# Column sums of the second attention layer as two float32r products in another PSUM bank, the next batch's half-size sums issued apart, and the first batch's copies all on ScalarE

## The chip, the cores and the metric

The kernel runs on one NeuronCore of a Trainium2 chip. The metric is the device time of one execution in microseconds (us), given as the median of several runs. Engines are named as the profile names them: PE is TensorE (PEld its weight loads), DVE is VectorE, ACT is ScalarE, POOL is GpSimd, and SP is the engine whose queue issues most DMAs.

## The reference, cut to what matters

The input x is (8, 32, 32, 512) in float32: 8 batches of N = 1024 tokens with C = 512 channels. Two layers follow one another, each with a residual and a GroupNorm of 32 groups ahead of it.

```python
# layer 0: 16 heads of 32
qkv = (_gn(x) @ w_qkv)                       # q, k, v: 512 columns each
attn = softmax((q * 32**-0.5) @ k.T)         # per head, 1024 x 1024
x = x + (attn @ v) @ w_proj + b_proj
# layer 1: 4 heads of 128, with relative position logits
q, k, v = _gn(x) @ Wq / sqrt(128), _gn(x) @ Wk, _gn(x) @ Wv
scores = q @ k.T + relative_logits(q, pos_emb_w, pos_emb_h)
x = x + (softmax(scores) @ v) @ Wo
```

All of it is in float32. A softmax needs, for each query, the sum of the exponentials over 1024 keys; these sums are what the first part of the change is about.

## The kernel before

Activations lie transposed, channels on the partitions (`x0T`, `x1T`, four chunks of 128 channels). The 512x512 weight products are done in a Winograd form of seven products in place of eight: `forms` (L324) makes four half-size sums of the activation (`f_...`, each a DVE operation over 128x1024 elements, L332 to L335), `Matrix.add_up` (L146) makes the matching sums of the weights (`prep_...`), and `seven` runs the products, always cut into quarters of 32 columns (L312, so 16 issues make one product of 512).

Two batches are in flight. In loop b `side_by_side` (L862) steps through the first layer's attention of batch b (`attention_0`: scores L532, exponential L540 on ACT, accumulation L551, sums of exponentials L562 on DVE) and, by a running cost, hands out pieces of the other work between its steps: the output product of batch b-1's first layer, of batch b-2's second, the projections of batch b-1's second layer, its attention, and the projections of batch b+1. The second layer's attention has cost 0, so that it runs in one piece inside one step of the first layer's attention. Only in the last loop, b = 7, where no batch comes after, are the first 32 of its 64 steps for batch 6 spread among first-layer steps; and in the round after it batch 7's second layer runs with nothing beside it. The loading and normalising of batch b+1 (`load`) is woven into the second layer's attention: from its fourth step on, a piece at every sixth (L970). Its last piece is `forms`.

`attention_1` (L637) goes through 64 steps a batch: 4 heads h, 2 halves c of the queries, 8 blocks j of 128 keys. A step puts the scores into a bank (`ps`: L647 in full precision, L648, the position part, in float32r), takes the exponential on ACT (L650), multiplies it by v into the accumulator (L659), and adds it to the running sum `es` on DVE (L668, L670). The products of a step and the accumulation of the step before alternate. After eight steps ACT copies the accumulator to `q` (L673), and `finish` makes the sums over the partitions, by one full-precision product of an all-ones matrix and `es` (L679), into one of the three banks that the scores and the accumulator also use. `normalise` copies it (L495, ACT), takes reciprocals by way of two transposes (L497 to L513, DVE), and multiplies (L517, POOL). A batch has eight such finishes: seven are issued within the next group's first step, the last at once.

[...] four hold the first layer's scores (tag `ps`), one its accumulator (`acc`), three are those of `bank`. The framework's list scheduler orders each engine's instructions from the program order and its estimates; `tc.issue_after` and `tc.keep_in_program_order` bind it where they stand.

The first batch is loaded apart (`load_first`, L719): rows come by DMA, PE transposes them, ACT and DVE copy the two halves of the tokens (h = 0, 1) into four chunks, DVE takes statistics of each chunk (L248, L249), `put_away` (L217) sends each chunk to DRAM for the residual, and `group_norm` takes the averages (L260 to L285 on DVE, the root L289 on POOL) and normalises in place (L292). `fetch` (L135) brings a 512x512 weight matrix for `add_up`; both it and the copies to DRAM are on SP's queue.

Of the kernel before, what the change touches and what calls it, by code (L numbers as in the profile page):

```python
# [9 lines left out]
F32 = mybir.dt.float32  # L10
F32R = mybir.dt.float32r
# [6 lines left out]
P = 128  # L18
# [9 lines left out]
def quick_path(  # L28
# [23 lines left out]
    nc = tc.nc  # L52
# [28 lines left out]
    def bank(name, shape=None):  # L81
        return psum.tile(shape or [P, NB], F32, tag="bank", name=name, bufs=3)
# [1 line left out]

    ident = consts.tile([P, P], F32, tag="ident", name="ident")
    make_identity(nc, ident)
    ones = consts.tile([P, P], F32, tag="ones", name="ones")
    nc.gpsimd.memset(ones, 1.0)
    bproj_sb = consts.tile([P, CC], F32, tag="bproj_sb", name="bproj_sb")
    with nc.allow_non_contiguous_dma(reason="512 values, once"):  # L90
        nc.gpsimd.dma_start(bproj_sb, b_proj.rearrange("(cc p) -> p cc", p=P))
# [212 lines left out]
    in_place = [False]  # L304

    half_done = [None]

    def by_columns(out, weights, moving, start, stop, open_sum=False):

# [11 lines left out]
                tc.keep_in_program_order(ins)  # L321
        in_place[0] = False

    def forms(x, name):  # L324


        a11, a12 = x[:, :HC, :NB], x[:, HC:, :NB]
        a21, a22 = x[:, :HC, NB:], x[:, HC:, NB:]
        s1, s2, s4 = [
            mem.tile([P, HC, NB], F32, tag=f"form{i}", name=f"f{i}_{name}", bufs=1) for i in (1, 2, 4)  # L330
        ]
        nc.vector.tensor_add(s1, a21, a22)  # L332
        nc.vector.tensor_sub(s2, s1, a11)  # L333
        nc.vector.tensor_sub(a21, a11, a21)
        nc.vector.tensor_sub(s4, a12, s2)  # L335
        return [a11, a12, s4, a22, s1, s2, a21]

    def snapshot(tag, name):
        return mem.tile([P, NB], F32, tag=tag, name=name, bufs=3 if tag == "e1" else 2)
# [294 lines left out]
                if i % 2:  # L634
                    yield 0

    def attention_1(q, k, v, posT, b):  # L637

        steps = [(h, c, j) for h in range(H1) for c in range(NH) for j in range(NT)]
        state = {}  # L640

        def front(h, c, j):
            name = f"1_{b}_{h}_{c}_{j}"
            ps = bank(f"ps_{name}")
            keys = slice(j * P, (j + 1) * P)
            queries = slice(c * NB, (c + 1) * NB)
            nc.tensor.matmul(ps, k[h][:, keys], q[:, h, queries], start=True, stop=False)  # L647
            nc.tensor.matmul(ps, sel_flat[:, keys], posT[:, h, queries], start=False, stop=True)  # L648
            e = mem.tile([P, NB], F32, tag="e1", name=f"e_{name}", bufs=3)
            nc.scalar.activation(e, ps, AF.Exp, scale=1.0 / math.sqrt(D1))  # L650
            return e

        def back(h, c, j, e):
            name = f"1_{b}_{h}_{c}_{j}"
            if j == 0:
                state["acc"] = bank(f"acc_{name}")
                state["first"] = e
            acc = state["acc"]
            nc.tensor.matmul(  # L659
                acc,  # L660
                v[:, j, h * D1 : (h + 1) * D1],
                e,
                start=(j == 0),
                stop=(j == NT - 1),
            )
            if j == 1:
                state["esum"] = mem.tile([P, NB], F32, tag="es1", name=f"es_{name}", bufs=2)
                nc.vector.tensor_add(state["esum"], state["first"], e)  # L668
            elif j > 1:
                nc.vector.tensor_add(state["esum"], state["esum"], e)  # L670
            if j < NT - 1:
                return
            nc.scalar.copy(q[:, h, c * NB : (c + 1) * NB], acc)  # L673
            state["ended"] = (h, c, state["esum"])

        def finish(h, c, esum):
            name = f"1_{b}_{h}_{c}"
            su = bank(f"sums_{name}")
            nc.tensor.matmul(su, ones, esum, start=True, stop=True)  # L679
            normalise(q[:, h, c * NB : (c + 1) * NB], su, name)  # L680

        pending = None
        for at in steps:
            e = front(*at)
            ended = state.pop("ended", None)
            if pending is not None:
                back(*pending)
            pending = (*at, e)
            if ended is not None:
                finish(*ended)  # L690
            yield 0
        back(*pending)
        yield 0
        finish(*state.pop("ended"))

    def load(b, st):

        x = xT = None
        parts = [(cc, h) for cc in range(CC) for h in range(NH)]
        ahead = [load_blocks(b, *parts[i]) for i in range(2)]  # L700
        for i, (cc, h) in enumerate(parts):
            xs = ahead.pop(0)
            if i + 2 < len(parts):
                ahead.append(load_blocks(b, *parts[i + 2]))
            if h == 0:
                yield 0
            if x is None:
                x = block(f"x0T_{b}")
                xT = chunks(x)
            nc.vector.transpose(xT[cc][:, h * NB : (h + 1) * NB], xs)  # L710
            if h == NH - 1:
                statistics(st, xT, cc, f"0_{b}")
        yield 0
        st["kept"] = put_away(xT, f"0_{b}")
        yield from group_norm(st, xT, f"0_{b}")
        st["xn"] = forms(x, f"xn0_{b}")
        yield 0

    def load_first(st):  # L719

        rows = block("x_rows", [P, NT, C])
        for t in range(NT):
            queue = nc.scalar if t % 2 else nc.sync
            queue.dma_start(rows[:, t, :], xf[0, t * P : (t + 1) * P, :])
        WV0.fetch(nc.sync)
        x = block("x0T_0")
        xT = chunks(x)
        for h in range(NH):
            if h == 0:
                whole = psum.tile([P, CC, NB], F32, tag="ps", name="turned_0", bufs=1)  # L730
                banks = [whole[:, cc, :] for cc in range(CC)]
            else:
                banks = [bank(f"turned_1_{cc}") for cc in range(CC - 1)]
                banks.append(psum.tile([P, NB], F32, tag="acc", name="turned_1", bufs=1))
            for t in range(NT // NH):
                for cc in range(CC):
                    nc.tensor.transpose(
                        banks[cc][:, t * P : (t + 1) * P],
                        rows[:, h * (NT // NH) + t, cc * P : (cc + 1) * P],
                        ident,  # L740
                    )
            for cc in range(CC):
                part = xT[cc][:, h * NB : (h + 1) * NB]
                if h == 0 or cc % 2:
                    nc.scalar.copy(part, banks[cc])
                else:
                    nc.vector.tensor_copy(part, banks[cc])

        idle = psum.tile([P, CC, NB], F32, tag="ps", name="idle", bufs=1)
        for t in range(6):  # L750
            nc.tensor.matmul(idle[:, t % CC, :], ident, rows[:, t, :], start=True, stop=True)
        for cc in (1, 0, 3, 2):
            statistics(st, xT, cc, "0_0")
        st["kept"] = put_away(xT, "0_0")
        run(group_norm(st, xT, "0_0"))
        st["xn"] = forms(x, "xn0_0")
# [101 lines left out]
    def run(part):  # L858
        for _ in part:
            pass  # L860
# [25 lines left out]
    def later(part, *args):  # L886

        yield from part(*args)
# [28 lines left out]
    WV0.add_up(nc.gpsimd, nc.gpsimd, keep=True)  # L917
    for m in (WQ0, WK0):
        m.fetch(nc.sync)
        m.add_up(nc.vector, nc.gpsimd, keep=True)  # L920
    fill_sel()
    stream = Stream(plan)

# [12 lines left out]
    for b in range(B + 1):  # L936
# [11 lines left out]
        if last is not None:  # L948
            norm = norm_1(b - 1, last, (lambda: half_done[0]) if past is not None else None)
            rest.append(after_0(b - 1, last, forms_past if past is not None else None))  # L950
            total += PRODUCT
            if past is not None:
                rest.append(woven(later(after_1, b - 2, past), norm, 3, 3))
                total += PRODUCT
            else:
                rest.append(chain([ALONE], (cost + ALONE for cost in norm), marked()))
                total += 4 * ALONE
            rest.append(later(second, b - 1, last))
            total += SECOND
            attention = later(lambda st: attention_1(*st.pop("at")), last)  # L960
            if here is not None and coming is None:

                attention = woven(
                    (int(at < H1 * NT) for at, _ in enumerate(attention)),
                    at_once(forms_0),
                    H1 * NT + NT,
                    H1 * NH * NT,
                )
                total += H1 * NT
            rest.append(woven(attention, incoming, 4, 6))  # L970
        else:
            rest.append(woven(rest_of_first(here), incoming, 0, 2))
            total += PRODUCT
# [502 lines left out]
```

## Time and profile before

| | |
|---|---|
| median of 9 runs | 3888.27 us (3885.27 to 3892.73) |
| the profiled execution | 3891.15 us, its span 3889.4 us |
| mean granted TensorE clock | 0.995 of full speed |
| PE busy | 3808.2 us, 98% of the span |
| DVE busy | 2514.8 us, 65% |
| ACT busy | 1724.4 us, 44% |
| POOL busy | 619.5 us, 16% |
| second-layer sums (L679) | 128 issues for 64 finishes |

The span is from the first to the last instruction of the profiled execution; the time holds what lies around it too. Busy shares are averages over stages with different limits. A group's line has the operation, its output and inputs with shapes, its count, the busy time and the mean of one in ns, and the idle time ahead of it with what ended it. A float32 product appears as two issues (x2) in the records. The records of PE overlap, since products are pipelined; the chain of waits cuts each piece where the next one starts.

### The profile page before, as it was taken

Reading aid. Unit: us, or ns where it says so; the run is one execution under the profiler, and the core shown is the slowest. Engines: PE = TensorE matmul, PEld = TensorE weight load, DVE = VectorE, ACT = ScalarE, POOL = GpSimd, SP = SyncE. Lnnn points to the kernel's source line nnn. Section 1 sums busy time; section 2 is a strip of 40 time slices with the busy share of each in tenths; the row PEclk is TensorE's granted clock in tenths of the full one; section 3 lists DMA queues with packets and bytes.
Section 4 is the critical chain, followed back from the end, with each engine's and each line's share of the span. In section 5 each row is a group of like instructions: output and inputs, shape, how many; then the busy total and the mean of one; then the engine's idle time right before and its main releaser. Section 6 shows DMA issues by size and latency. Waiting matters only on the chain. (4 is left out here: it accounts for less than half of the span.)

```text
span 3889.4 us, 79819 instructions
## 1 busy us (share of the span) xinstructions
PE 3808.2 (98%) x34478; PEld 1371.3 (35%) x34478; DVE 2514.8 (65%) x2905; ACT 1724.4 (44%) x1767; POOL 619.5 (16%) x400
## 2 busy tenths in 40 slices
PE   8999899999999999999999999999999999999998
PEld 3222244232442324432344323433234332334353
DVE  5767775577745867458674586646866568665544
ACT  2554553445434454344544445444453445553132
POOL 1341001121111210113110121111211112001101
PEclk9999999999999999999999999999999999999999
DMA  5231120133201422023220231202411033111401
GB/s 170 76 107 42 47 61 6 39 116 69 62 2 42 122 65 57 7 80 91 53 55 13 92 90 40 52 20 93 93 41 41 25 96 76 33 43 34 121 18 23
DMA packets 482984, 234.73 MB, mean 60 GB/s; under 512 B 269600, under 2 KB 461376, under 8 KB 481600
## 3 DMA queue, kind: packets, MB, share of 16 engines
q1 hardware_dynamic: 470992, 213.74, 20.4%
q0 software_dynamic: 2608, 13.70, 1.0%
q8 instruction: 274, 4.49, 0.5%
q10 hardware_dynamic: 9024, 2.10, 0.3%
q14 instruction: 86, 0.70, 0.1%
HBM read 170.72 MB, written 58.72 MB: 59 GB/s over the span
## 5 line engine op out<-in xcount | busy, mean ns | idle before, releaser
L540 ACT ACTIVATE e<-ps 128x2048 f32<-128x2048 f32 x512 | 961.6, 1878 | 838.2 <-PE ps L532 624.6
L562 DVE TENSOR_TENSOR es<-es,e 128x2048 f32<-128x2048 f32 x384 | 891.7, 2322 | 422.6 <-ACT e L540 419.9
L532 PE MATMUL ps<-q,k 32*64 32x512 f32 x8192 | 578.5, 617 | 27.1 <-ACT e L540 27.1
L650 ACT ACTIVATE e<-ps 128x512 f32<-128x512 f32 x512 | 305.7, 597 | 572.6 <-PE ps L648 539.2
L551 PE MATMUL acc<-e,v 128*32 128x512 f32 x4096 | 547.8, 606 | 0.0
L647 PE MATMUL ps<-q,k 128*128 128x512 f32 x1024 | 525.2, 594 | 0.3 <-DVE posT L633 0.3
L659 PE MATMUL acc<-e,v 128*128 128x512 f32 x1024 | 522.0, 593 | 0.0
L517 POOL TENSOR_TENSOR q<-q,su 128x512 f32<-128x512 f32 x128 | 213.4, 1668 | 1596.3 <-DVE su L513 1551.6
L670 DVE TENSOR_TENSOR es<-es,e 128x512 f32<-128x512 f32 x384 | 290.9, 758 | 250.9 <-ACT e L650 248.8
L648 PE MATMUL ps<-posT,sel 128*128 128x512 f32 x512 | 406.8, 795 | 0.0
L647 PEld LDWEIGHTS ps<-q,k 128*128 128x128 f32 x1024 | 192.9, 190 | 250.8 <-issue 244.5
L532 PEld LDWEIGHTS ps<-q,k 32*64 32x64 f32 x8192 | 120.5, 130 | 422.0 <-issue 220.4
L659 PEld LDWEIGHTS acc<-e,v 128*128 128x128 f32 x1024 | 193.5, 190 | 146.4 <-issue 105.1
L551 PEld LDWEIGHTS acc<-e,v 128*32 128x32 f32 x4096 | 81.8, 108 | 414.2 <-issue 368.2
L560 DVE TENSOR_TENSOR es<-e,e 128x2048 f32<-128x2048 f32 x64 | 173.9, 2717 | 38.0 <-ACT e L540 38.0
L497 DVE STREAM_TRANSPOSE tu<-su 128x512 f32<-128x512 f32 x128 | 90.6, 708 | 128.1 <-ACT su L495 128.0
L495 ACT COPY su<-sums 128x512 f32<-128x512 f32 x128 | 74.9, 585 | 150.4 <-PE sums L572 78.2
L648 PEld LDWEIGHTS ps<-posT,sel 128*128 128x128 f32 x512 | 97.5, 190 | 122.3 <-issue 122.3
L633 DVE TENSOR_TENSOR posT<-pp,posT 32x512 fp32r<-32x512 f32 x128 | 112.0, 875 | 32.0 <-ACT posT L628 30.7
L668 DVE TENSOR_TENSOR es<-e,e 128x512 f32<-128x512 f32 x64 | 44.2, 690 | 134.8 <-ACT e L650 134.8
L421 POOL TENSOR_TENSOR k<-b_k,p_k 128x512 f32<-128x512 f32 x32 | 51.2, 1600 | 482.0 <-ACT p_k L386 479.9
L628 ACT CAST posT<-pp 32x512 fp32r<-32x512 f32 x128 | 105.9, 827 | 45.9 <-PE pp L615 44.8
(195 smaller groups left out, 4454.2 us busy)
## 6 DMA issues: line engine op xcount, KB each, us to landing
w_qkv<-ws_qkv SPq DMA_DIRECT2D x168, 128.0 KB, 2.5
d<-x0T SPq DMA_DIRECT2D x32, 512.0 KB, 3.5
x1T<-d SPq DMA_DIRECT2D x32, 512.0 KB, 5.4
d<-x1T SPq DMA_DIRECT2D x32, 512.0 KB, 3.6
x2T<-d SPq DMA_DIRECT2D x32, 512.0 KB, 6.5
w_qkv<-in_L_conv_w_qkv SPq DMA_DIRECT2D x126, 128.0 KB, 2.2
out<-ot SPq DMA_DIRECT2D x240, 64.0 KB, 2.0
xs<-in_x SPq DMA_DIRECT2D x224, 64.0 KB, 2.5
```

The costliest lines, as they stand in the source:

```text
L517: nc.gpsimd.tensor_tensor(dst, dst, su, op=ALU.mult)
L532: nc.tensor.matmul(ps[some, r, :], k[m][rows, j * P + 64 * i : j * P + 64 * i + 64], q[m][rows, h * NB : (h + 1) * NB], start=True, stop=True,
L540: nc.scalar.activation(e, ps, AF.Exp, scale=D0 ** -0.5)
L551: nc.tensor.matmul(acc[r * D0 : (r + 1) * D0, :], v[:, j, c0 : c0 + D0], e[:, r, :], start=(j == 0), stop=(j == NT - 1),)
L560: nc.vector.tensor_add(state["esum"], state["first"], e)
L562: nc.vector.tensor_add(state["esum"], state["esum"], e)
L633: nc.vector.tensor_sub(rest, logits, greater)
L647: nc.tensor.matmul(ps, k[h][:, keys], q[:, h, queries], start=True, stop=False)
L648: nc.tensor.matmul(ps, sel_flat[:, keys], posT[:, h, queries], start=False, stop=True)
L650: nc.scalar.activation(e, ps, AF.Exp, scale=1.0 / math.sqrt(D1))
L659: nc.tensor.matmul(acc, v[:, j, h * D1 : (h + 1) * D1], e, start=(j == 0), stop=(j == NT - 1),)
L670: nc.vector.tensor_add(state["esum"], state["esum"], e)
```

## The change

Inside `attention_1` a finish becomes a generator. Its first part, issued right after the step in which the group's last addition stands, splits the running sum: ACT copies it rounded to float32r (`sg`), DVE subtracts that from it (`sr`). Three steps later two float32r products with the ones add `sg` and `sr` up, in the first of the four banks of the tag `ps`; `normalise` follows as before. At the end of a batch all parts run at once. Where the first layer's attention is stepped beside (the first 32 steps of batch 6), the first three finishes keep the old product and bank; they are now issued one place earlier, ahead of the next step's products.

`forms` is also to be had as a generator, `forming`. `load` uses it, each of the four sums a piece of its own, bound to be issued behind the newest addition to `es`; and since there are three more pieces, they are woven in at every fifth step for every sixth.

In `load_first` all copies go to ACT, in the order of chunks 0, 2, 1, 3, and the statistics follow that order. The weight sums of two matrices on DVE are bound behind the last of the first batch's half-size sums. In the built program this also moves a fetch of 1 MB (`prep_qkv`) ahead of the four copies to DRAM on SP's queue.

```diff
@@ -84,8 +84,9 @@
 
     ident = consts.tile([P, P], F32, tag="ident", name="ident")
     make_identity(nc, ident)
-    ones = consts.tile([P, P], F32, tag="ones", name="ones")
-    nc.gpsimd.memset(ones, 1.0)
+    ones_r = consts.tile([P, P], F32R, tag="ones", name="ones")
+    nc.gpsimd.memset(ones_r.bitcast(F32), 1.0)
+    ones = ones_r.bitcast(F32)
     bproj_sb = consts.tile([P, CC], F32, tag="bproj_sb", name="bproj_sb")
     with nc.allow_non_contiguous_dma(reason="512 values, once"):
         nc.gpsimd.dma_start(bproj_sb, b_proj.rearrange("(cc p) -> p cc", p=P))
@@ -304,6 +305,9 @@
     in_place = [False]
 
     half_done = [None]
+    last_form = [None]
+
+    added = [None]
 
     def by_columns(out, weights, moving, start, stop, open_sum=False):
 
@@ -321,7 +325,7 @@
                 tc.keep_in_program_order(ins)
         in_place[0] = False
 
-    def forms(x, name):
+    def forming(x, name, behind=None):
 
 
         a11, a12 = x[:, :HC, :NB], x[:, HC:, :NB]
@@ -329,11 +333,27 @@
         s1, s2, s4 = [
             mem.tile([P, HC, NB], F32, tag=f"form{i}", name=f"f{i}_{name}", bufs=1) for i in (1, 2, 4)
         ]
-        nc.vector.tensor_add(s1, a21, a22)
-        nc.vector.tensor_sub(s2, s1, a11)
-        nc.vector.tensor_sub(a21, a11, a21)
-        nc.vector.tensor_sub(s4, a12, s2)
+        for op, out, one, other in (
+            (nc.vector.tensor_add, s1, a21, a22),
+            (nc.vector.tensor_sub, s2, s1, a11),
+            (nc.vector.tensor_sub, a21, a11, a21),
+            (nc.vector.tensor_sub, s4, a12, s2),
+        ):
+
+            late = behind() if behind is not None else None
+            with tc.issue_after(late.ins) if late is not None else nullcontext():
+                last_form[0] = op(out, one, other)
+            yield 0
         return [a11, a12, s4, a22, s1, s2, a21]
+
+    def forms(x, name):
+        got = []
+
+        def whole():
+            got.append((yield from forming(x, name)))
+
+        run(whole())
+        return got[0]
 
     def snapshot(tag, name):
         return mem.tile([P, NB], F32, tag=tag, name=name, bufs=3 if tag == "e1" else 2)
@@ -634,7 +654,7 @@
                 if i % 2:
                     yield 0
 
-    def attention_1(q, k, v, posT, b):
+    def attention_1(q, k, v, posT, b, beside=0):
 
         steps = [(h, c, j) for h in range(H1) for c in range(NH) for j in range(NT)]
         state = {}
@@ -667,7 +687,7 @@
                 state["esum"] = mem.tile([P, NB], F32, tag="es1", name=f"es_{name}", bufs=2)
                 nc.vector.tensor_add(state["esum"], state["first"], e)
             elif j > 1:
-                nc.vector.tensor_add(state["esum"], state["esum"], e)
+                added[0] = nc.vector.tensor_add(state["esum"], state["esum"], e)
             if j < NT - 1:
                 return
             nc.scalar.copy(q[:, h, c * NB : (c + 1) * NB], acc)
@@ -675,23 +695,43 @@
 
         def finish(h, c, esum):
             name = f"1_{b}_{h}_{c}"
-            su = bank(f"sums_{name}")
-            nc.tensor.matmul(su, ones, esum, start=True, stop=True)
+            if (h * NH + c + 1) * NT < beside:
+                su = bank(f"sums_{name}")
+                nc.tensor.matmul(su, ones, esum, start=True, stop=True)
+                normalise(q[:, h, c * NB : (c + 1) * NB], su, name)
+                return
+
+            yield
+
+            greater = mem.tile([P, NB], F32R, tag="rec", name=f"sg_{name}", bufs=2)
+            nc.scalar.copy(greater, esum)
+            rest = mem.tile([P, NB], F32R, tag="rec", name=f"sr_{name}", bufs=2)
+            nc.vector.tensor_sub(rest, esum, greater.bitcast(F32))
+
+            yield
+            yield
+
+            su = psum.tile([P, HB, NB], F32, tag="ps", name=f"sums_{name}", bufs=1)[:, 0, :]
+            nc.tensor.matmul(su, ones_r, greater, start=True, stop=False)
+            nc.tensor.matmul(su, ones_r, rest, start=False, stop=True)
             normalise(q[:, h, c * NB : (c + 1) * NB], su, name)
 
         pending = None
+        ending = []
         for at in steps:
             e = front(*at)
-            ended = state.pop("ended", None)
             if pending is not None:
                 back(*pending)
             pending = (*at, e)
-            if ended is not None:
-                finish(*ended)
+            for part in ending:
+                next(part, None)
+            if "ended" in state:
+                ending = [finish(*state.pop("ended"))]
+                next(ending[0], None)
             yield 0
         back(*pending)
         yield 0
-        finish(*state.pop("ended"))
+        run(finish(*state.pop("ended")))
 
     def load(b, st):
 
@@ -713,8 +753,7 @@
         yield 0
         st["kept"] = put_away(xT, f"0_{b}")
         yield from group_norm(st, xT, f"0_{b}")
-        st["xn"] = forms(x, f"xn0_{b}")
-        yield 0
+        st["xn"] = yield from forming(x, f"xn0_{b}", lambda: added[0])
 
     def load_first(st):
 
@@ -739,17 +778,14 @@
                         rows[:, h * (NT // NH) + t, cc * P : (cc + 1) * P],
                         ident,
                     )
-            for cc in range(CC):
+            for cc in (0, 2, 1, 3):
                 part = xT[cc][:, h * NB : (h + 1) * NB]
-                if h == 0 or cc % 2:
-                    nc.scalar.copy(part, banks[cc])
-                else:
-                    nc.vector.tensor_copy(part, banks[cc])
+                nc.scalar.copy(part, banks[cc])
 
         idle = psum.tile([P, CC, NB], F32, tag="ps", name="idle", bufs=1)
         for t in range(6):
             nc.tensor.matmul(idle[:, t % CC, :], ident, rows[:, t, :], start=True, stop=True)
-        for cc in (1, 0, 3, 2):
+        for cc in (0, 2, 1, 3):
             statistics(st, xT, cc, "0_0")
         st["kept"] = put_away(xT, "0_0")
         run(group_norm(st, xT, "0_0"))
@@ -917,7 +953,9 @@
     WV0.add_up(nc.gpsimd, nc.gpsimd, keep=True)
     for m in (WQ0, WK0):
         m.fetch(nc.sync)
-        m.add_up(nc.vector, nc.gpsimd, keep=True)
+
+        with tc.issue_after(last_form[0].ins):
+            m.add_up(nc.vector, nc.gpsimd, keep=True)
     fill_sel()
     stream = Stream(plan)
 
@@ -957,8 +995,11 @@
                 total += 4 * ALONE
             rest.append(later(second, b - 1, last))
             total += SECOND
-            attention = later(lambda st: attention_1(*st.pop("at")), last)
-            if here is not None and coming is None:
+            shared = here is not None and coming is None
+            attention = later(
+                lambda st, steps: attention_1(*st.pop("at"), steps), last, H1 * NT if shared else 0
+            )
+            if shared:
 
                 attention = woven(
                     (int(at < H1 * NT) for at, _ in enumerate(attention)),
@@ -967,7 +1008,7 @@
                     H1 * NH * NT,
                 )
                 total += H1 * NT
-            rest.append(woven(attention, incoming, 4, 6))
+            rest.append(woven(attention, incoming, 4, 5))
         else:
             rest.append(woven(rest_of_first(here), incoming, 0, 2))
             total += PRODUCT
```

## Prediction

> **What bounds the kernel now.** I read the page's busy times first, then the windows inside the second layer's attention, the products by shape, the chain that ended last, and the timeline where one batch's attention ends. From the page:
>
> ```profile
> PE 3808.2 (98%) x34478; PEld 1371.3 (35%) x34478; DVE 2514.8 (65%) x2905; ACT 1724.4 (44%) x1767; POOL 619.5 (16%) x400
> ```
>
> TensorE is 98% of the span. Where the change acts it is everything (a window's TensorE busy us stand twice after its limits):
>
> ```profile
> 600.00:700.00 100.00, 100.00 (x351) 45.17 (x349) 47.06 (x76) 37.02 (x58) 9.07 (x6) 1.00 0.02 5
> ```
>
> The groups by shape show no idle ahead of any second-layer product worth naming (last number of the first three):
>
> ```profile
> L659 PE MATMUL acc<-e,v 128*128 128x512 f32 x1024 | 522.0, 593 | 0.0
> L648 PE MATMUL ps<-posT,sel 128*128 128x512 f32 x512 | 406.8, 795 | 0.0
> L679 PE MATMUL sums<-es,ones 128*128 128x512 f32 x128 | 65.4, 592 | 0.0
> ...
> L633 DVE TENSOR_TENSOR posT<-pp,posT 32x512 fp32r<-32x512 f32 x128 | 112.0, 875 | 32.0 <-ACT posT L628 30.7
> ...
> L495 ACT COPY su<-sums 128x512 f32<-128x512 f32 x128 | 74.9, 585 | 150.4 <-PE sums L572 78.2
> ```
>
> Records overlap, so prices come from the chain, where each piece runs to the next one's start (columns: start, us):
>
> ```profile
> 3734.66 0.23 PE ps L648
> 3734.89 0.86 PE acc L659 x2
> 3735.75 0.86 PE sums L679 x2
> 3736.61 0.86 PE ps L647 x2
> ```
>
> A full-precision product of 512 columns is two issues and 0.857 us; the float32r product L648 is one issue and 0.23. A step is 0.857 + 0.231 + 0.857 = 1.945, and every eight steps 0.857 more for sums. So time here is a count of TensorE issues, and only two things count: a cheaper product, or a wait the idle engines newly make. Last the end of batch 0's second-layer attention:
>
> ```profile
> 684.52 1.97 PE L659 MATMUL acc<-e,v 128*128 128x512 f32 x4
> ...
> 685.35 0.69 DVE L670 TENSOR_TENSOR es<-es,e 128x512 f32<-128x512 f32 x1 [1.26 <-ACT e L650]
> ...
> 686.09 0.43 PEld L679 LDWEIGHTS sums<-es,ones 128*128 128x128 f32 x2 [0.43 <-DVE es L670]
> 686.33 1.02 PE L679 MATMUL sums<-es,ones 128*128 128x512 f32 x2
> 686.53 0.58 ACT L673 COPY q<-acc 128x512 f32<-128x512 f32 x1 [1.22 <-PE acc L659]
> 687.28 0.16 PEld L312 LDWEIGHTS x_q<-x0T,w_qkv 128*32 128x32 f32 x8 [0.76 <-issue]
> 687.28 1.92 PE L312 MATMUL x_q<-x0T,w_qkv 128*32 128x512 f32 x16
> ```
>
> There the sums' weights wait for the last addition: little slack is left at a batch's end.
>
> [...]
>
> **The change part by part.**
>
> *Sums inside a batch.* Of 64 second-layer finishes 3 keep the old form (batch 6's first three, inside the loop shared with the first layer), 8 are the last of their batch, 53 lie inside. Each of these gives up one full-precision product and gets two float32r ones: 0.857 − 2 × 0.231 = 0.40 us. [...] 53 × 0.40 = **−21.2 us** (−20.7 to −22.8), if nothing waits.
>
> New on ACT is the copy of the sums, which stands between exponentials 7 and 8 and waits for the last addition. Nothing here shows an SBUF-to-SBUF copy of 128x512; [...] ACT's copy from PSUM takes 0.585, the slowest float32r writer (L628, with permuted writes) 0.83. I take 0.60. Addition 7 ends 0.72 after exponential 7, the copy would end some 0.06 + 0.59 later, at 1.38; exponential 8 starts 1.35 after 7 today, so it slips by 0.03, and its accumulation has 0.92 of slack. Queued behind the copy are exponential 8 and, after it, the accumulator's copy; both stay inside that slack. The subtraction on DVE (0.69 as an addition, 0.875 if priced by L633) is needed three steps, 5.8 us, later. The sums' bank is one that the first layer's attention uses; no first-layer step runs meanwhile. Cost 0; with addition 7 late by one half-size sum (1.2, or 2.28 beside POOL), about 0.4 or 1.5 us of PE wait each time.
>
> *Half-size sums of the next batch.* All four stood in the third group of eight steps, the fourth directly ahead of addition 7, which then ended 2.06 after its exponential. In the changed order they stand after addition 3 of the sixth group, after 7 of the sixth, after 5 of the seventh and after 2 of the eighth. None is directly ahead of an addition 7, so that wait stays covered; the second one does delay that group's subtraction by 1.2 to 2.3, inside its 5.8. TensorE waited for none of them before: 0. The incoming pieces are spaced at 5 for 6; its DMAs and their waits on SP move by some steps of 1.9 us in a batch of 124 us and 0.02 DMA share: 0.
>
> *Batch ends (8).* The finish runs at once. Addition 7 ends at 686.04; the copy ends near 686.68; the subtraction near 687.43; the second float32r product then has its operand, and x_q starts near 687.43 + 0.3 (semaphore and weight load) + 0.23 + 0.07 = 688.03 for 687.28. The order puts a lone quarter of the next product into this gap, but a lone quarter that elsewhere issued alone took 0.95 instead of 0.21 as one of sixteen, so it fills the wait and saves nothing. +0.75 each, 7 × 0.75 = **+5.25**; at 0.83 and 0.875 for copy and subtraction +0.43 more each. The last batch's end is a bare chain (sums, su, DVE, POOL's multiply, f_ao, the last y_wo): +0.75, POOL's gather for the last output now ahead of that multiply +1.0, an addition between the two f_ao sums +0.65, the first f_ao no longer beside POOL −1.05: **+1.3**.
>
> *Batch 6's shared part.* Two old-form finishes are now ordered directly after the last accumulation, with a lone piece of the first layer's scores split off ahead of them: 2 × 0.86 = 1.7, and a DVE transpose ahead of 2.29-us additions 0.3: **+2.0** (0 to +4).
>
> *Start.* ScalarE makes all eight copies of the first batch and statistics follow in that order; they end about 4.9 us sooner (DVE's wait of 1.74 for prepared weights and four weight sums of 0.65 move from ahead of them). But on SP's queue the 1-MB weight fetch goes ahead of the four copies to DRAM (these landed at 18.2, 19.5, 20.9 and 22.2; the fetch at 27.6, DMA 0.95 busy). Normalising a chunk overwrites what its copy reads, so with that fetch ahead I put the landings near 21 to 27 and normalising at about its old 25.0–28.0. Eight weight sums, 8 × 0.65 = 5.2 us, now stand on DVE between the half-size sums and a_v, which TensorE wants at 34.85: it moves to some 38, with 36 further quarter products of 0.107 = 3.9 us to cover it. On POOL the root now precedes a weight store. I take **−0.5** (−4.8 if the landings don't matter, +3 if a_v does).
>
> *Sum.* −21.2 + 5.25 + 1.3 + 2.0 − 0.5 = −13.1. The profiled execution took 3891.15 with a span of 3889.4, so 1.75 lies around it; the new span is 3876.3, that execution 3878.0. Against the median of the runs, 2.88 below that execution, this is 3888.27 − 13.1 = **3875.2 us**, −0.34%. What a measurement here can tell from no change is 0.2%, 7.8 us: faster is below 3880.5, slower above 3896.0.
>
> **Rivals.**
>
> *Ends eat the gain.* Every batch end costs 2.2 us for 0.75 (a copy that is slow, a subtraction behind other DVE work, an order of the next products that is no longer in sixteens), so 8 × 1.45 = 11.6 more: 3887, no difference. For: a wait of 0.43 is there already, two engines are added in series. Against: the next products need neither result. Chance 0.12.
>
> *ScalarE stalls the accumulation: slower.* The copy at the head of ACT's queue holds exponential 8 until addition 7 is done. Beyond 0.82 us of lateness the PE waits at acc. If DVE is busy with a 2.28-us piece (a half-size sum, a layer-0 addition, a statistics piece) exposure is about 1.5. The gain is gone at 13.1/53 = 0.25 us a finish; slower by 0.2% needs (13.1 + 7.8)/53 = 0.40. At 28 finishes of 1.5 it gives +42 − 13 = +29, 3917. For: DVE is 65% busy, and the third groups of six batches had this lateness. Against: the changed order has no long sum directly ahead of addition 7, and DVE is 47% busy in that window. Chance 0.06.
>
> *The float32r product isn't quarter price* with the ones as weights: at 0.43 the pair equals the old product, and ends and start remain: 3888.3 + 8.1 = 3896.4. L648 at 0.23 speaks against. Chance 0.03.
>
> *Start pays and ends are free.* The waits at the ends hide and the earlier statistics carry through: −21.2 + 2 − 4 = −23, 3865. For it: the copies' tails are short. Against: 0.95 DMA. Chance 0.08.
>
> **How the numbers follow.** My case has 0.71, its own range 3870 to 3881 (slow copy and subtraction +3.4; start −4.3 to +3.5; shared part ±2; product price −1.6). The end and start rivals stretch this to 3869 to 3883, leaving out the far ends of both. Faster: 0.71 less a twentieth, plus 0.08 and part of the first rival: 0.80. Same: 0.13. Slower: 0.07.
>
> **What would show it.** Right: 6 issues left of the sums' 128 in full precision, and 122 float32r ones of 0.23 in the chain; a period of 16.0 for 16.43 between equal steps; PE at 100.00 in inner windows; exponential 8 about 1.4 after exponential 7. The ends: x_q 2.7 after exponential 7's end for 1.96 (685.32 to 687.28), with a wait put down to DVE's subtraction. Start: first x_v near 26, a_v near 38 without a PE wait above 0.5. Wrong: PE waits at acc put down to ACT's exponential, a wait of several us at a_v or x_v, or idle at the ends above 1 us.

## The result, and the profile after

The changed kernel takes 3875.46 us (median of 10 runs, 3872.69 to 3880.0) against 3888.55 us (median of 30 runs) for the kernel before: a ratio of 0.9968, 95% interval 0.9961 to 0.9976, or 13.1 us less. The prediction was 3875.2 us. The profiled execution took 3879.23 us with a span of 3877.4; it is one of the longer runs of its kernel, so below stages are compared, not spans.

From the page:

```profile
PE 3799.4 (98%) x34478; PEld 1375.8 (35%) x34478; DVE 2559.4 (66%) x2964; ACT 1762.0 (45%) x1830; POOL 612.0 (16%) x400
```

The products by shape (after the bar: busy us, mean ns, idle before), and the window that was shown of before:

```profile
L679 PE MATMUL acc<-e,v 128*128 128x512 f32 x1024 | 521.9, 593 | 0.0
L668 PE MATMUL ps<-posT,sel 128*128 128x512 f32 x512 | 406.6, 794 | 0.0
L715 PE MATMUL sums<-sg,ones 128*128 128x512 f32 x61 | 46.3, 758 | 0.0
L716 PE MATMUL sums<-sr,ones 128*128 128x512 f32 x61 | 24.4, 401 | 0.0
L700 PE MATMUL sums<-es,ones 128*128 128x512 f32 x6 | 3.3, 627 | 0.0
```

```profile
600.00:700.00 100.00, 100.00 (x386) 45.06 (x384) 52.01 (x81) 42.42 (x65) 10.04 (x7) 1.00 0.03 7
```

Three finishes are left in the old form (6 issues), 61 are new; the records show no idle time ahead of any (at a batch's end a small piece of the next product lies in the wait, see below), and TensorE still has no gap in the window. So the gain there is cheaper work, as the chain of waits shows (start and duration in us):

```profile
575.98 0.86 PE acc L679 x2
576.84 0.23 PE sums L715
577.07 0.23 PE sums L716
577.30 0.86 PE ps L667 x2
```

0.23 and 0.23 stand where 0.86 stood. The second layer's attention of batch 1, from its first score product to its last accumulation, took 130.38 us before and takes 127.67: 2.71 over seven groups, 0.387 each. Below, this stretch is called the batch's inner attention.

What pays for it on the other engines is seen in the timeline behind the last step of a group. Here exponential 7 ended at 568.83:

```profile
568.87 0.69 DVE L690 TENSOR_TENSOR es<-es,e 128x512 f32<-128x512 f32 x1 [1.25 <-ACT e L670]
569.59 0.62 ACT L707 CAST sg<-es 128x512 fp32r<-128x512 f32 x1 [0.76 <-DVE es L690]
569.98 1.02 PE L679 MATMUL acc<-e,v 128*128 128x512 f32 x2
570.24 0.60 ACT L670 ACTIVATE e<-ps 128x512 f32<-128x512 f32 x1
570.31 0.69 DVE L709 TENSOR_TENSOR sr<-es,sg 128x512 fp32r<-128x512 f32 x1 [0.76 <-ACT sg L707]
```

Exponential 8 starts 1.41 after exponential 7's end for 1.35, and what is left ahead of its accumulation is 0.86 for 0.92. At the end of batch 0 the same split stands bare:

```profile
681.96 0.62 ACT L707 CAST sg<-es 128x512 fp32r<-128x512 f32 x1 [0.81 <-DVE es L690]
682.25 1.04 PE L316 MATMUL x_q<-x0T,w_qkv 128*32 128x512 f32 x2
...
682.68 0.69 DVE L709 TENSOR_TENSOR sr<-es,sg 128x512 fp32r<-128x512 f32 x1 [0.81 <-ACT sg L707]
683.23 0.51 PE L715 MATMUL sums<-sg,ones 128*128 128x512 f32 x1
683.57 0.40 PE L716 MATMUL sums<-sr,ones 128*128 128x512 f32 x1
683.90 1.49 PE L316 MATMUL x_q<-x0T,w_qkv 128*32 128x512 f32 x11
```

The rest of x_q starts 2.75 after exponential 7's end (681.15) for 1.96 before. A lone quarter at 682.25 (two of the product's 16 issues) lies in the wait and saves nothing: in batch 1, where the same happens, the other 14 issues take 1.84 us, and all 16 took 1.85 before. At the last batch's end POOL's order is the new one:

```profile
3836.24 1.28 POOL L451 TENSOR_TENSOR x2T<-x2T,p_wo 128x512 f32<-128x512 f32 x1 [8.80 <-issue]
...
3837.48 1.27 POOL L537 TENSOR_TENSOR q<-q,su 128x512 f32<-128x512 f32 x1
3838.78 1.22 DVE L345 TENSOR_TENSOR f_ao<-q 128x1024 f32<-128x1024 f32 x1 [2.31 <-POOL q L537]
3839.92 0.68 DVE L456 TENSOR_TENSOR x2T<-x_wo,x2T 128x512 f32<-128x512 f32 x1
3840.52 1.21 DVE L345 TENSOR_TENSOR f_ao<-f_ao,q 128x1024 f32<-128x1024 f32 x1
3841.79 3.64 PE L316 MATMUL y_wo<-f_ao,w_o 128*32 128x512 f32 x16 [3.66 <-DVE f_ao L345]
```

Multiply behind the x2T addition, first f_ao 1.22 without POOL beside it (2.27 in the kernel before, where POOL's addition to x2T of 1.26 ran beside it), an addition before the second: y_wo starts 10.99 after exponential 7's end, 9.70 before. (That its 16 issues last 3.64 is another matter: the granted clock was half from 3840.2 to 3847.0 in this execution.)

### The profile page after: what moved, and what is told of

It reads as the page before. It is cut to its first block, busy times and chain, and to the rows that moved or that the text cites. A ratio compares the mean times of both kernels' runs of the same rounds, so it can differ in the third digit from the quotient of the medians.

```text
span 3877.4 us, 79880 instructions
## 1 busy us (share of the span) xinstructions
PE 3799.4 (98%) x34478; PEld 1375.8 (35%) x34478; DVE 2559.4 (66%) x2964; ACT 1762.0 (45%) x1830; POOL 612.0 (16%) x400
## 4 chain that ended last, share of the span: by engine, by line
PE 86%; DVE 8%; ACT 3%; issue 2%; DMA 1%; SPq 0%; POOL 0%; DVEq 0%; ACTq 0%; POOLq 0%
PE ps L552 12%; PE ps L667 11%; PE acc L679 11%; PE acc L571 11%; PE y_k L316 4%; PE y_v L316 4%; PE y_q L316 4%; PE ps L668 3%; PE x_q L316 3%; PE x_k L316 3%; PE x_v L316 3%; PE z_k L316 3%; PE z_q L316 3%; PE z_v L316 3%; ACT e L560 2%; DVE es L582 2%
## 5 line engine op out<-in xcount | busy, mean ns | idle before, releaser
L441 POOL TENSOR_TENSOR v<-b_v,p_v 128x512 f32<-128x512 f32 x32 | 50.8, 1587 | 443.0 <-ACT p_v L406 440.4
```

## The experiments

All of them were run beside the kernel before on the same chip. Line numbers in a kernel's profile are its own.

### The batch ends with the old product

```diff
-            if (h * NH + c + 1) * NT < beside:
+            if (h * NH + c + 1) * NT < beside or h * NH + c + 1 == H1 * NH:
```

> The changed kernel, but the last finish of each batch keeps the full-precision product. My theory: seven batch ends cost 0.78 us each in the changed kernel's trace and the last one 0.76 of sums, with POOL's gather put ahead of its multiply on top; with the old product there x_q starts 1.96 after exponential 7's end again instead of 2.76, and the kernel gains 6 to 8 us on the changed one: 3868 to 3870. Rival, the lone quarter of the next product that is put into the gap does useful work, so the ends cost nothing: 3875 as the changed kernel.

Measured: 3869.82 us (5 runs), ratio 0.9951 (0.9937 to 0.9964). The traces agree with the price: from the last accumulation to the first layer's next score product this kernel needs 0.77 to 0.78 less than the changed kernel at each of the batches 0 to 5. So the ends do cost what was worked out, and the lone quarter does no useful work.

### The start alone

The first batch's part of the change on the kernel before; its sums and half-size sums stay as they were.

> The kernel before with the start's part of the change alone (copies on ScalarE, statistics' order, weight sums bound behind the half-size sums). My theory: the first product starts 4.4 us sooner, but the fourth chunk's normalising waits for its copy to DRAM until about 26.8, and the early products run at half clock; the first attention starts 1 to 2 us sooner: 3886.5 to 3887.5, within 0.2% of before. Rival, the earlier statistics carry through: 3884.

Measured: 3886.32 us (13 runs) beside 3887.88 of before, ratio 0.9994 (0.9985 to 1.0002): 1.6 us, not to be told from none, and by itself no proof against the rival's 3.9 either. The traces decide: the first attention starts at 77.11 here, for 78.05 before. Over the eight traces with this start it comes at 76.48 to 77.13, over the three with the old one at 78.05 to 79.07, on average 1.7 us later. The rival falls.

The half clock of these early products isn't what eats the start's gain. From 21 to 31 us (PE busy twice, PEld, DVE, ACT, POOL, then the clock) the first line is the changed kernel, the second this one:

```profile
21.00:31.00 10.00, 8.26 (x72) 2.86 (x76) 6.15 (x7) 1.04 (x2) 0.00 (x0) 0.50 0.94 280
21.00:31.00 10.00, 6.08 (x68) 2.15 (x72) 5.84 (x7) 1.17 (x2) 0.00 (x0) 0.75 0.94 283
```

This kernel had half clock for about half as long in the window (a mean of 0.75 for 0.50) and reached the first attention no sooner (77.11 for 76.48): TensorE waited more instead (busy 6.08 for 8.26). The chain of waits of the changed kernel (start and duration in us) shows for what:

```profile
13.73 13.07 DMA d<-x0T
...
26.83 0.82 DVE x0T L293
...
32.43 3.68 DVE prep_qkv L147 x7
...
37.25 0.61 DVE a_v L392
...
37.90 2.13 PE y_v L316 x33
```

Up to 37.90 it runs through the last copy to DRAM, that chunk's normalising, the half-size sums, the weight sums and a_v; TensorE's products are not on it.

### The half-size sums in one piece again

```diff
-        st["xn"] = yield from forming(x, f"xn0_{b}", lambda: added[0])
+        st["xn"] = forms(x, f"xn0_{b}")
+        yield 0
...
-            rest.append(woven(attention, incoming, 4, 5))
+            rest.append(woven(attention, incoming, 4, 6))
```

> The changed kernel, but the next batch's half-size sums as before, one piece, incoming pieces at every sixth step. My theory: in the built order none of the four stands directly ahead of an addition 7 here either, two additions lie between; no exponential 8 is held up and the time is that of the changed kernel, 3875.5 within 3. Rival, the spreading of these sums is what keeps addition 7 on time now that the ScalarE copy waits for it: a group in each of six batches shows exponential 8 late by 1.3 to 2.3 beyond exponential 7 and PE waits at the accumulation, 0.4 to 1.5 each: 3878 to 3885.

Measured: 3885.09 us (13 runs), 9.6 more than the changed kernel. My expectation was wrong, the rival's mechanism right. Waits of TensorE (us in all, times, longest), then the timeline of one group whose exponential 7 ended at 597.65:

```profile
PE acc L679 <- ACT e L670: 7.2, 6, 1.2
```

```profile
597.10 2.29 DVE L345 TENSOR_TENSOR f_xn<-x0T,f_xn 128x1024 f32<-128x1024 f32 x1
...
599.32 1.48 DVE L690 TENSOR_TENSOR es<-es,e 128x512 f32<-128x512 f32 x2
...
600.88 0.62 ACT L707 CAST sg<-es 128x512 fp32r<-128x512 f32 x1 [3.23 <-DVE es L690]
601.40 0.59 ACT L670 ACTIVATE e<-ps 128x512 f32<-128x512 f32 x1
...
602.05 1.12 PE L679 MATMUL acc<-e,v 128*128 128x512 f32 x2 [1.14 <-ACT e L670]
```

Two additions do lie between the half-size sum and the copy (the line of DVE at 599.32 holds both). But the sum takes 2.29 with POOL's multiply (596.75 to 598.31) beside it, for 1.21 of the same sum in the kernel before, so both additions start late and run one behind the other; the copy ends 3.85 after exponential 7, exponential 8 starts at 3.76 instead of 1.41, and TensorE waits. Six groups, one in each of batches 0 to 5, are 1.40 to 1.48 longer: some 8.7 of the 9.6 us.

### The sums alone

The third experiment with the old start as well: only the part that the change is named after.

> The kernel before with only the sums as two float32r products: half-size sums in one piece, incoming pieces at every sixth step, start as before. My theory, from the traces: 53 groups give 0.387 each (20.5), seven batch ends take 0.78, the last one's chain 1.3, the shared part 2.4, and six groups in which a half-size sum stands ahead of additions 6 and 7 take 1.45 each (8.7): 2.7 us faster than before, not to be told from it: 3885 to 3887.5. Rival, the half-size sums hurt only together with the changed start: 3876 to 3879.

Measured: 3886.48 us (21 runs), ratio 0.9992 (0.9985 to 0.9999), inside the expected range. Its trace has the same six waits of 7.2 us in all. A batch's inner attention, 2.71 shorter in the changed kernel, is 1.22 to 1.33 shorter here in the batches 0 to 5, and 0.78 of this goes at its end.

### The half-size sums alone

> The kernel before with only the half-size sums apart, each behind an addition, and incoming pieces at every fifth step. My theory: before, ScalarE does not wait for addition 7, so a late one reaches nothing that TensorE needs; alone the part is worth nothing: 3888 within 3. Rival, the four sums cost TensorE time in the kernel before as well: 3879 to 3883.

Measured: 3889.81 us (13 runs), ratio 1.0001 (0.9993 to 1.0009). Worth nothing in the kernel before, some 9 us with the new sums: the part keeps addition 7 on time, and only the copy on ScalarE made that matter. The three parts alone have the ratios 0.9992, 1.0001 and 0.9994, together 0.9968: most of the gain needs the sums and the spreading at once.

### Late additions, two operations

```diff
             yield
 
+            if h * NH + c + 1 < H1 * NH:
+                for _ in range(2):
+                    nc.vector.tensor_tensor(esum, esum, esum, op=ALU.max)
             greater = mem.tile([P, NB], F32R, tag="rec", name=f"sg_{name}", bufs=2)
```

> The changed kernel with two more DVE operations of 128x512 (the larger of the sum and itself, so nothing changes in the value) between addition 7 and the ScalarE copy in each finish inside a batch, 56 less the three old ones. This is the rival by which the kernel would have been slower, made to happen. My theory: the copy ends near 2.8 instead of 1.43 after exponential 7, exponential 8 starts 1.4 later, 0.86 of this is slack, so each of 53 groups lasts some 0.5 us longer: +25 to +32, 3900 to 3908. If the slack were larger than the trace shows, or ACT ran exponential 8 first: 3876.

Measured: 3876.57 us (7 runs), no loss. The expectation was missed, but the run didn't test the slack: in the built order exponential 8 stands ahead of the copy, so that it starts 1.35 after exponential 7 with its full 0.92 of slack while the copy ends at 2.88. A late copy costs nothing in this order.

### The same, with exponential 8 held behind the copy

For the first step of a group the exponential is issued with `tc.issue_after(held[0].ins)`, where `held[0]` is the copy; to make that possible the split is issued one step earlier in the program. One and two extra operations.

> Two extra DVE operations did nothing because ScalarE ran exponential 8 ahead of the copy there. Here exponential 8 is bound behind the copy in the 53 finishes inside a batch, with one extra DVE operation between addition 7 and the copy. My theory: the copy ends near 2.15 after exponential 7, exponential 8 starts 0.75 later than in the kernel before, inside its 0.92 of slack: the time of the changed kernel, 3873 to 3879. Rival, any lateness of exponential 8 reaches TensorE: 53 by some 0.7 us, 3912.

> As hold1, with two extra DVE operations; ScalarE's order also has the accumulator's copy between the copy of the sums and exponential 8. My theory: exponential 8 starts near 3.5 after exponential 7 for 1.35, 0.92 of the 2.15 is slack, each of 53 groups is 1.1 to 1.3 us longer: +58 to +69 on the changed kernel, 3934 to 3945. Rival, the wait is made up for within the group, since the later steps have slack of their own: 3876.

Measured: 3887.11 us (12 runs) with one, 3906.63 us (4 runs), ratio 1.0046 (1.003 to 1.0061), with two. Both expectations missed in size, and the traces say why. With one, exponential 8 starts 2.06 after exponential 7 and has 0.21 of slack left; batch 7's inner attention is as long as in the changed kernel (0.00 over seven groups), so the slack is real. The traces place some 9 of the 11.6 us. In each of batches 0 to 5 one group is 1.18 longer: there a half-size sum stands behind addition 7 and now lies ahead of the extra operation and thus of the copy. In batches 1 to 5 another, with a statistic of the next batch in that place, is 0.24 longer; batch 6 is 0.57 longer and the last end 0.33. What is left is no more than the intervals of the two ratios allow. With two, one of batch 7's groups reads:

```profile
3756.97 1.42 DVE L714 TENSOR_TENSOR es<-es 128x512 f32<-128x512 f32 x2
...
3758.42 0.62 ACT L715 CAST sg<-es 128x512 fp32r<-128x512 f32 x1 [2.21 <-DVE es L714]
...
3759.31 0.40 PE L724 MATMUL sums<-sg,ones 128*128 128x512 f32 x1
3759.42 1.09 ACT L673 ACTIVATE e<-ps 128x512 f32<-128x512 f32 x2
3759.89 0.50 PE L725 MATMUL sums<-sr,ones 128*128 128x512 f32 x1 [0.18 <-DVE sr L717]
3760.23 1.02 PE L686 MATMUL acc<-e,v 128*128 128x512 f32 x2
```

In most groups exponential 8 is 1.92 late (1.86 in this one), 1.00 beyond its slack, but the built order has the two products of the sums in this wait (3.10 after exponential 7 for 7.45), which fills 0.46 of it. What is left measures 0.48 a group (3.37 over batch 7's seven). That is the prediction's stall on ScalarE, made to happen: a copy held late in all groups makes the kernel slower than before.

### The best version: old ends, old place in the shared part

```diff
             if (h * NH + c + 1) * NT < beside or h * NH + c + 1 == H1 * NH:
+                if h * NH + c + 1 < H1 * NH:
+                    yield
```

> As ends_old (the last finish of each batch in full precision), and the three old-form finishes of batch 6's shared part issued one step later again, as in the kernel before. My theory: with the lone pieces of the first layer's scores gone and the sums behind the next accumulation, the shared part's 2.4 us come back: 3866 to 3868.5. Rival, those 2.4 us are not of the order but of the clock: 3869.8 as ends_old.

Measured: 3868.94 us (5 runs), ratio 0.9942 (0.9929 to 0.9956). The trace of batch 6, from its first score product to its last accumulation, is 2.39 us shorter than that of the first experiment. The medians differ by 0.9, which their spread of 5 us doesn't resolve.

### The order of SP's queue at the start

The 1-MB weight fetch bound behind the four copies to DRAM, once on the best version, once on the changed kernel.

```diff
-        m.fetch(nc.sync)
+        with tc.issue_after(last_put[0].ins) if m is WK0 else nullcontext():
+            m.fetch(nc.sync)
```

> As best, with the 1-MB weight fetch bound behind the four copies to DRAM on SP's queue. My theory: the copies land by about 23 instead of 26.8, the fourth chunk is normalised some 3 us sooner, but a_v, behind eight weight sums of which four wait for that fetch, becomes the wait, and the half clock covers the early products; the first attention starts 0 to 1.5 us sooner: 3867 to 3869. Rival, the fetch comes late for the weight sums and a_v, and TensorE waits 2 us or more before 45: 3871.

> The changed kernel with one step of it undone: the 1-MB weight fetch goes behind the four copies to DRAM on SP's queue again, as in the kernel before. With best under it this moved the first attention 4.1 us ahead in the trace and the median by 7.9. Theory: the fourth chunk's normalising starts near 22 instead of 26.8, TensorE's first products no longer stand at half clock until 31, and the first attention starts 3.5 to 4.5 us sooner than in the changed kernel; the median falls by 4 to 8: 3867.5 to 3871.5. Rival, the gain under best was a chance of the clock: first attention within 1 us of the changed kernel's, 3874 to 3877.

Measured: 3861.01 us on the best version, ratio 0.9927 (0.9914 to 0.9941), the fastest kernel of the study; on the changed kernel 3871.93 us, ratio 0.9959 (0.9946 to 0.9973), 3.5 less than without it. The first expectation forecast too small a gain, the second a little too large a one (4 to 8 us for 3.5). The copies land from 18.1 to 21.8 for 20.5 to 26.8, and the first attention starts 4.1 us (on the changed kernel 3.2) sooner, and a_v, which was expected to become the wait, comes at 32.81 without one. So the order of the queue is what held the start back. The waits of DVE in the first 40 us (us in all, times, longest), of the changed kernel and of it with this step undone:

```profile
DVE x0T L293 <- DMA d<-x0T: 5.4, 4, 2.7
```

```profile
DVE x0T L293 <- POOL rstd L290: 1.2, 1, 1.2
```

With the fetch ahead, each chunk's normalising waits for its copy; with it behind, for the root alone. The other 4 us of the gain on the best version do not stem from the start: between 76 and 330 us its trace has no stretch of half clock, where the best version's has three of 3.41, and its lead grows from 4.1 to 10.7 us there. Whether that follows from the earlier start or is chance isn't settled; on the changed kernel the same edit gained nothing beyond the start.

## Why the prediction was right

By its own steps, measured in place of predicted:

| step | predicted | measured | where |
|---|---|---|---|
| sums inside, 53 finishes | −21.2 | −20.5 | 0.387 each, seven groups of batch 1 |
| seven batch ends | +5.25 | +5.4 | 0.78 each, against the kernel with old ends |
| last end | +1.3 | +1.29 | exponential 7's end to y_wo, 10.99 for 9.70 |
| batch 6's shared part | +2.0 | +2.4 | traces of the best version and of that with old ends |
| half-size sums | 0 | 0 | alone 1.0001 (0.9993 to 1.0009) |
| start | −0.5 | −1.6 | first attention 76.48 for 78.05; alone 0.9 in its trace, 1.6 by the medians |
| sum | −13.1 | −13.0 | medians: −13.1 |

The sum is nearer than its terms. Inside, 0.7 less was saved than forecast (just outside the range I had estimated), the shared part and the ends cost 0.4 and 0.15 more, and the start gave 1.1 more; that these cancel is luck. The mechanism of the largest terms, cheaper products inside and a bare wait at the ends, is what the traces show.

*Inside.* The saving measured is 0.387 for 0.40, so that a pair of the new products costs 0.47 for 0.46; the copy took 0.62 for 0.60 (my estimate, next to the 0.585 measured for ScalarE's copy from PSUM), the subtraction 0.69, exponential 8 slipped by 0.06 for 0.03.

*Ends.* The sum of copy, subtraction and one product was right to 0.04 us. The trace doesn't put the wait down to DVE's subtraction, as I wrote, but to ScalarE's copy of the accumulator, ahead of the first product's weight load. The subtraction is done at 683.37, just before the second's weight load at 683.42; no wait for it is listed.

*Half-size sums.* "None is directly ahead of an addition 7, so that wait stays covered" held, and the price of losing the cover, about 1.5 beside POOL, measured 1.45. What I didn't see is that being directly ahead is not needed: in the old arrangement two additions stand between and the wait comes all the same. In the expectation for it I used the order where the durations were wanted.

*Shared part.* Mis-sized by 0.4; shown by putting the old order back.

*Start.* The result is near, but the step is wrong in its inside. I had normalising "at about its old 25.0–28.0" and x_v near 26. Normalising began at 20.6, each chunk waited for its copy, the fourth until 26.83, and x_v started at 21.5. TensorE thus began 4.4 us sooner and kept 1.6, because the fourth chunk and the DVE work behind it, up to a_v, set when y_v could start. The landings near 21 to 27 were right. a_v came at 37.17, near the 38 forecast, and TensorE stood idle for less than 0.1 us there, as forecast. With the fetch behind the copies the start gave 4.75 us (first attention 73.30 for 78.05), the 4.8 that I had named for landings that don't matter.

*Rivals.* That ends eat the gain falls at 0.78 an end for 2.2; that they are free falls with it. The stall on ScalarE exists: it took 1.45 in each of six groups in two runs and 0.48 a group where exponential 8 was held; in the changed kernel it takes nothing. The quarter price stands, roughly: 0.23 for 0.86.

## What to carry to other kernels

A full-precision sum over partitions can be split into a float32r part and its remainder, two float32r products at 0.47 for 0.86 us, where two more engines have time for the split (0.62 on ScalarE, 0.69 on VectorE) and the consumer can wait; at a point where nothing else can run, the old product was the faster (0.78 us an end). An operation that is set ahead of a critical one in the order of an engine makes its producer's lateness critical: with the copy ahead of exponential 8 and the addition it waits for late, the exponential started 3.76 after exponential 7 for 1.41; with the copy behind it, a copy that ended at 2.88 cost nothing. Find the slack (0.92 here), then list by duration, and not by order alone, what can make the producer late. Two parts that gave 3 us and nothing apart gave some 11 us together here (13.1 less the start's 1.6), so parts have to be measured together too. And where data are overwritten in place, what is queued ahead of their copy to DRAM belongs to the path: here the last copy landed at 26.8 with the fetch ahead of it, at 21.8 with the fetch behind.

## What was not expected of the hardware

In the thirteen traces kept here every stretch of half clock that ends before the kernel does lasts 3.41, 6.83 or 10.24 us: in the kernel before 10.24 from 21.24, then 3.41 five times and 6.83 once; in the changed kernel 10.24 from 20.70, then 3.41 twice, 6.83 twice and 10.24 once. At the start they add up to 10.24 us in eight of them, the kernel before among these, to 6.83 in four and to 3.41 in one. The order of SP's queue doesn't settle which: with the fetch behind the copies it was 3.41 to 10.24, with it ahead 6.83 to 10.24. What does settle it isn't shown.

Later in the kernel the stretches come in different places from one trace to the next: in the kernel before at 106.58, 178.26, 219.22, 348.92, 400.12 and 3646.20, in the changed kernel at 106.03, 215.26, 344.96, 396.16 and 3840.21. The runs of the changed kernel have mean granted clocks of 0.994 to 0.996 with the same code, so two profiled executions can differ by some us without a cause in it: the changed kernel's trace had such a stretch at y_wo (the one at 3840.21), and from there to the end it took 35.65 us for 33.00 before.
